# Layer 1's projections formed inside layer 0's finish, and the branch to the general path placed behind layer 1

## The chip, the cores and the metric

The kernel runs on one core of one Trainium2 chip. The metric is the device time of one execution in microseconds (us), and less is better. A core has a matrix engine (TensorE, "PE" in the profile, with "PEld" for its weight loads), VectorE (DVE), ScalarE (ACT), GpSimd (POOL) and a sequencer for transfers (SyncE, "SP"). Each engine works through its own queue in order, and the engines wait for each other by semaphores. Transfers (DMA) are issued from the queues of SP, ACT and POOL.

## The reference

There are N = 2708 nodes with D = 256 features and a weighted adjacency matrix `adj`. Two layers follow each other, and each is wrapped as `x = layernorm(x + layer(x))`.

Layer 0 walks two steps over the graph and attends two steps with nucleus sparsification:

```
R = (S + I) / rowsum
for n in 0, 1:
    A  = top-p attention of Xa          # softmax(q k^T), the fewest entries with 0.9 of the mass, renormalised
    Xf = R @ Xf
    Xa = A @ Xa
    Z  = Z + Xf @ U1[n].T + Xa @ U2[n].T
out = layernorm(X + Z) * g + b
```

Layer 1 is graph attention with H = 4 heads of 64 features each:

```
Wh  = x @ W                      # per head
s_i = Wh . a_src,  s_j = Wh . a_dst
e   = leaky_relu(s_i + s_j, 0.2),  only where adj != 0 or i == j
out = softmax_j(e) @ Wh
```

The kernel writes exp(leaky_relu(s_i + s_j)) as a product: exp(s_j) times the larger of exp(0.8 s_i) and exp(-0.8 s_j), leaving out a factor that the softmax cancels. So layer 1 needs, for each node j, the values `Wh` scaled by exp(s_j), the number exp(s_j) itself for the denominator, the number `tj` = exp(-0.8 s_j), and the source score s_i.

## The kernel before

The nodes are cut into NT = 22 tiles: 16 of 128 rows and 6 of 110 rows. The features of all nodes lie in `xe` in SBUF for the whole run. Everything is in 32-bit floats.

**Layer 0** is `fast_layer0`. It runs step 0 and then step 1 of attention, one row tile after the other, in the function `step`. For each row tile, `weigh` (line 132) goes over six groups of up to four tiles: it transposes a group of the attention row on TensorE into the PSUM buffer `tr` (pool `ps_tr`, two buffers), copies it on ScalarE to `eT`, and multiplies it with the values (line 157). After each group, `slot` lets other work in. It first advances the searches for coming rows (`going`), then the tails of earlier rows (`doing`), and then spends a number of matmuls on the walk `R @ Xf` (line 783). The order of the four compute engines inside this part is the order in which the Python code emits it (`tc.manual_schedule`). The order on SP, and the place of everything outside that region, are chosen by the framework's list scheduler, which goes by program order and by its own estimate of when things are ready.

A search for row tile t (`search`) computes the scores and their exponentials, finds a threshold with tallies on ScalarE (line 583) and small arithmetic on GpSimd, and on VectorE picks candidates (line 663), sorts them and cuts the row `e` (line 732).

The tail of a row tile in step 1 is `finish` (lines 848 to 883). It sums the terms on GpSimd, applies two layernorms (VectorE and GpSimd in turn), and writes the new features into `xe` (line 873). It is a generator; each `yield` gives the engines a slot.

After layer 0 a number `bad` tells whether the fast search was valid for every row. Line 1030 loads it into a register of each engine, and a branch (line 1031) enters `general_layer0` if it is positive. With these inputs the branch is not entered. A conditional block splits the program: nothing traced behind it can be scheduled ahead of it.

**Layer 1** begins with a loop of its own over the 22 tiles (lines 1053 to 1081). Per tile it makes two transposes of `xe` (line 1060), a copy on ScalarE (line 1064), two matmuls with `wx` (W and the two score vectors side by side, 264 columns, line 1067), two exponentials on ScalarE (lines 1072 and 1073), a copy and a product on VectorE (lines 1076 and 1077) and a copy on GpSimd that spreads exp(s_j) over 32 columns (`bj`, line 1081). `targets(g)` (lines 1089 to 1104) turns the source scores of a span of eight tiles into the rows `r`. `neighbours(g, j)` loads a block of `adjT`, and makes a mask of zeros and ones with ScalarE (Sign, line 1112), GpSimd (two products on the diagonal block, lines 1115 and 1116) and ScalarE again (Square, line 1117). The main loop runs over three spans and 22 tiles j: four VectorE instructions make `pt` (line 1164), and TensorE multiplies them with `v` (line 1172) and with `bj` (line 1179) into six PSUM banks. At the end of a span `settle` divides, adds `xe` and applies the last layernorm.

Pools of SBUF and PSUM are stacked. A pool of layer 1 lies on bytes of released pools of layer 0, and the framework lets all of its tiles wait for every user of the pools on whose bytes it lies. In layer 0 the pools stand in this order: `w0` (weights), `rowp` (small per-row buffers, among them `xT` and `cs`, two buffers each), `keep`, `sortp`, `heldp` (with `hh`, which `finish` uses), `finp`, `ep` and others. In layer 1 they are `keep1` (`v`, `bj`; it lies on `w0`, `rowp` and the start of `keep`), `pp`, `rp` (`r`; by its size it ends on `heldp`), `adjp1` (the blocks `bar`; on `heldp`, `finp` and `ep`) and `pj` (`pt`).

Of the kernel before, what the change touches and what calls it, by code (L numbers as in the profile page):

```python
# [45 lines left out]
def kernel(  # L46
# [36 lines left out]
    const = ctx.enter_context(tc.tile_pool(name="const", bufs=1))  # L83
# [24 lines left out]
    nc.vector.tensor_scalar(offdiag, ident, -1.0, 1.0, op0=ALU.mult, op1=ALU.add)  # L108
    minus_half = const.tile([P, 1], F32, name="minus_half")
    nc.gpsimd.memset(minus_half, -0.5)  # L110
    bad = const.tile([1, 1], I32, name="bad")

    def load_x():
# [4 lines left out]
    def layernorm(dst, src, m):  # L118

        st = small.tile([P, 6], F32, name="ln_st")  # L120
        nc.vector.bn_stats(st[:m], src)
        mv = small.tile([P, 2], F32, name="ln_mv")
        nc.vector.bn_aggr(mv[:m], st[:m])
        ve = small.tile([P, 1], F32, name="ln_ve")
        nc.gpsimd.tensor_scalar(ve[:m], mv[:m, 1:2], LN_EPS, None, op0=ALU.add)  # L125
        rs = small.tile([P, 1], F32, name="ln_rs")
        nc.gpsimd.tensor_tensor(rs[:m], ve[:m], minus_half[:m], op=ALU.pow)
        nc.vector.tensor_scalar(  # L128
            dst, src, mv[:m, 0:1], rs[:m], op0=ALU.subtract, op1=ALU.mult
        )  # L130

    def weigh(acc, e, m, value, pool, ps, copies, between=None):

# [31 lines left out]
    def general_layer0():  # L165
        with ExitStack() as l0:
# [232 lines left out]
            for s in range(STEPS):  # L399
                cur = xe if s == 0 else xa1  # L400
                ahead = scores(s, 0)
                for t in range(NT):
                    m = rows[t]
                    e, tau = ahead
                    if t + 1 < NT:
                        ahead = scores(s, t + 1)
                    if s == 0:
                        xf, xa = xf1[:, t, :], xa1[:, t, :]
                    else:
                        xf = rowp.tile([P, D], F32, name="xf2")  # L410
                        xa = rowp.tile([P, D], F32, name="xa2")
                    walk(s, t, xf[:m])
                    rden = top_p(t, e, tau)
                    attend(t, e, rden, cur, xa[:m])
                    if s == 0:
                        project(1, t, xa)
                    else:
                        finish(t, xf, xa)


    def fast_layer0():
# [426 lines left out]
        def finish(t, ac, ca, cb):  # L848

            m = rows[t]  # L850
            xt = xe[:m, t, 0:D]
            xw = rowp.tile([P, D], F32, name="xw")[:m]
            nc.scalar.activation(xw, ac[:m, :D], AF.Copy, scale=rinv[:m, t : t + 1])  # L853
            yield
            while t not in held:
                yield
            hh = heldp.tile([P, D], F32, name="hh", bufs=4)[:m]
            nc.gpsimd.tensor_add(ca[:m], ca[:m], cb[:m])
            nc.gpsimd.tensor_add(ca[:m], ca[:m], held.pop(t)[:m])
            nc.gpsimd.tensor_add(hh, ca[:m], xw)  # L860
            yield
            for last in range(2):
                st, mv = small.tile([P, 6], F32, name="ln_st")[:m], small.tile([P, 2], F32, name="ln_mv")[:m]
                nc.vector.bn_stats(st, hh)
                nc.vector.bn_aggr(mv, st)
                yield
                yield
                ve, rs = new("ln_ve", m), new("ln_rs", m)
                nc.gpsimd.tensor_scalar(ve, mv[:, 1:2], LN_EPS, None, op0=ALU.add)
                nc.gpsimd.tensor_tensor(rs, ve, minus_half[:m], op=ALU.pow)  # L870
                yield
                yield
                nc.vector.tensor_scalar(
                    xt if last else hh, hh, mv[:, 0:1], rs, op0=ALU.subtract, op1=ALU.mult
                )
                yield
                yield
                if not last:
                    nc.gpsimd.tensor_mul(hh, hh, g_sb[:m])
                    nc.gpsimd.tensor_add(hh, hh, b_sb[:m])  # L880
                    nc.gpsimd.tensor_add(hh, hh, xt)
                    yield
                    yield


        engines = {nc.tensor.engine, nc.scalar.engine, nc.vector.engine, nc.gpsimd.engine}
# [139 lines left out]
        )  # L1026
        l0.close()

    fast_layer0()
    flag = nc.values_load(bad[0:1, 0:1])  # L1030
    with tc.If(flag > 0):
        general_layer0()

    with ExitStack() as l1:  # L1040
        keep = l1.enter_context(tc.tile_pool(name="keep1", bufs=1))
        pp = l1.enter_context(tc.tile_pool(name="pp", bufs=2))
        GT = 8
# [1 line left out]
        GW = GT * rows[0]  # L1045


        v = keep.tile([P, NT, H, FO], F32, name="v")
        bj = keep.tile([P, NT, H, 32], F32, name="bj")
        tj = keep.tile([P, NT, H], F32, name="tj")  # L1050
        s_src = keep.tile([P, NT, H], F32, name="s_src")

        with ExitStack() as pre:
            ps_x = pre.enter_context(tc.tile_pool(name="ps_x", bufs=2, space=PSUM))
            ps_w = pre.enter_context(tc.tile_pool(name="ps_w", bufs=2, space=PSUM))
            for t in range(NT):
                m = rows[t]
                tp = ps_x.tile([P, DC, P], F32, name="tp")
                for c in range(DC):
                    nc.tensor.transpose(  # L1060
                        tp[:, c, :m], xe[:m, t, c * P : (c + 1) * P], ident[:m, :m]
                    )
                xT = pp.tile([P, DC, P], F32, name="xT")
                nc.scalar.copy(xT[:, :, :m], tp[:, :, :m])
                wp = ps_w.tile([P, D + 2 * H], F32, name="wp")
                for c in range(DC):
                    nc.tensor.matmul(
                        wp[:m], xT[:, c, :m], wx[:, c, :],
                        start=(c == 0), stop=(c == DC - 1),
                    )  # L1070
                b = small.tile([P, H], F32, name="b_j")
                nc.scalar.activation(b[:m], wp[:m, D : D + H], AF.Exp)
                nc.scalar.activation(
                    tj[:m, t, :], wp[:m, D : D + H], AF.Exp, scale=NEG_SLOPE - 1.0
                )
                nc.vector.tensor_copy(s_src[:m, t, :], wp[:m, D + H : D + 2 * H])
                nc.vector.tensor_tensor(
                    v[:m, t], wp[:m, 0:D].rearrange("p (h o) -> p h o", h=H),
                    b[:m].unsqueeze(2).to_broadcast([m, H, FO]), op=ALU.mult,
                )  # L1080
                nc.gpsimd.tensor_copy(bj[:m, t], b[:m].unsqueeze(2).to_broadcast([m, H, 32]))

        rp = l1.enter_context(tc.tile_pool(name="rp", bufs=2))
        adjp = l1.enter_context(tc.tile_pool(name="adjp1", bufs=4))
# [61 lines left out]
        for g, span in enumerate(spans):  # L1146
# [6 lines left out]
            for j in range(NT):  # L1153
                k = rows[j]
                if j == 2 and due:
                    settle(*due)
                if j == NT // 2 and g + 1 < len(spans):
                    r_next = targets(g + 1)
                mask = neighbours(g, j)
                at = dict(start=(j == 0), stop=(j == NT - 1), skip_group_check=True)  # L1160
                pts = []
                for h in range(H):
                    pt = pj.tile([P, GW], F32, name=f"pt{h}")
                    nc.vector.scalar_tensor_tensor(  # L1164
                        pt[:k, :gw], r[:k, h, :gw], tj[:k, j, h : h + 1], mask,
                        op0=ALU.max, op1=ALU.mult,
                    )
                    pts.append(pt)
                    if h % 2 == 1:
                        for c, (c0, w) in enumerate(cuts):  # L1170
                            for q in range(2):
                                nc.tensor.matmul(  # L1172
                                    acc[h // 2][c][q * FO : (q + 1) * FO, :w],
                                    v[:k, j, h - 1 + q, :],
                                    pts[h - 1 + q][:k, c0 : c0 + w], **at,
                                )
                for c, (c0, w) in enumerate(cuts):
                    for h in range(H):
                        nc.tensor.matmul(  # L1179
                            acc[2][c][h * 32 : (h + 1) * 32, :w],  # L1180
                            bj[:k, j, h, :], pts[h][:k, c0 : c0 + w], **at,
                        )
            r = r_next
            val = pp.tile([P, 2, GW], F32, name="val")
# [4 lines left out]
                nc.scalar.copy(den[:, c0 : c0 + w], acc[2][c][:, :w])  # L1189
            due = (g, val, den)  # L1190
        settle(*due)


# [43 lines left out]
```

## Time and profile before

Three runs gave 1730.11, 1731.68 and 1733.36 us. The profiled execution took 1728.95 us, and its span from first to last instruction is 1727.2 us.

| engine | busy us | share of the span |
|---|---|---|
| PE (matmuls) | 1622.7 | 94% |
| DVE | 1230.5 | 71% |
| ACT | 752.6 | 44% |
| POOL | 441.6 | 26% |

The shares are means over stages with different limits. The stages follow each other like this (times from the timeline):

| stage | from us | to us |
|---|---|---|
| layer 0, step 0 and the change to step 1 | 0 | 671 |
| layer 0, step 1, up to the last row's cut attention row | 671 | 1280 |
| layer 0, last row's attention and its finish | 1280 | 1306 |
| branch | 1306 | 1310 |
| layer 1, own loop over tiles | 1310 | 1347 |
| layer 1, main loop | 1347 | 1708 |
| layer 1, last settle and end | 1708 | 1727 |

A line of the timeline has: start in us, duration in us, engine, line of the code, operation, output<-inputs, shape, and how many instructions of that kind were merged into it; in square brackets, how long the engine had been idle and what ended that. A letter q behind an engine (DVEq, SPq) means its sequencer: waits, branches, DMA issues. A table of windows has, for each stretch: its length, the busy time of PE, PEld, DVE, ACT and POOL with the number of instructions, the granted TensorE clock, the DMA share and GB/s. A line of the waits has: who waited, for whom, the sum in us, how often, the longest.

### The profile page before, as it was taken

To read this page: it belongs to the slowest core of one execution; us is meant where nothing else is said; L and a number is where in the kernel's file an instruction comes from. 1 tells how busy PE (TensorE), PEld (TensorE's weight loads), DVE (VectorE), ACT (ScalarE), POOL (GpSimd) and SP (SyncE) were. 2 spreads that over 40 slices of the span, in tenths; PEclk is the share of its full clock that TensorE was granted. 3 is DMA by queue.
4 is the path that set the end of the run, shared out by engine and by line. 5 is a ranking of instruction groups with operands and counts; after the bars stand their busy time and mean duration, and the time that the engine had idled before them with its cause. 6 is when DMAs were issued, how large, how long until landed. Compare 5 with 4: busy or idle time off the path is not lost. (4 is left out here: it accounts for less than half of the span.)

```text
span 1727.2 us, 24421 instructions
## 1 busy us (share of the span) xinstructions
PE 1622.7 (94%) x8434; PEld 1075.6 (62%) x8434; DVE 1230.5 (71%) x3725; ACT 752.6 (44%) x1235; POOL 441.6 (26%) x915
## 2 busy tenths in 40 slices
PE   5799999999999998999999999999886999999896
PEld 4577777777777776777787877777675322222332
DVE  2654455554455009888989999999972888898796
ACT  1233333333332236666675666566514343333231
POOL 0011111111110124323343434343433200430303
PEclk9999999999999999999999999999998999999998
DMA  6111011111111142222232233232201232232231
GB/s 161 33 45 48 22 42 42 42 30 36 42 39 42 41 106 65 58 63 58 73 81 74 77 77 78 71 73 54 63 16 51 74 89 88 83 98 79 69 87 36
DMA packets 147812, 108.34 MB, mean 63 GB/s; under 512 B 39254, under 2 KB 138034, under 8 KB 147682
## 3 DMA queue, kind: packets, MB, share of 16 engines
q1 hardware_dynamic: 142018, 99.11, 21.6%
q0 software_dynamic: 2112, 5.55, 0.9%
q10 hardware_dynamic: 3552, 2.07, 0.5%
q8 instruction: 68, 1.11, 0.3%
q14 instruction: 62, 0.51, 0.1%
HBM read 98.38 MB, written 8.32 MB: 62 GB/s over the span
## 5 line engine op out<-in xcount | busy, mean ns | idle before, releaser
L1164 DVE SCALAR_TENSOR_TENSOR pt<-r,tj,bar 128x1024 f32<-128x1024 f32 (+3 forms) x264 | 295.9, 1181 | 29.2 <-issue 19.0
L583 ACT ACTIVATE junk<-e,minus,rth 128x2708 bf16<-128x2708 f32 (+1 forms) x88 | 232.8, 2645 | 39.8 <-POOL rth L615 36.6
L783 PE MATMUL walk<-xe,blk 128*128 128x257 f32 (+3 forms) x968 | 243.1, 385 | 0.0
L157 PE MATMUL att<-xe,eT 128*128 128x256 f32 (+3 forms) x968 | 233.4, 381 | 7.6 <-ACT eT L148 7.6
L157 PE MATMUL att<-ba,eT 128*128 128x256 f32 (+3 forms) x968 | 234.1, 383 | 5.0 <-ACT eT L148 5.0
L783 PE MATMUL walk<-yw,blk 128*128 128x256 f32 (+3 forms) x968 | 229.3, 383 | 4.0 <-ACT xw L853 4.0
L1172 PE MATMUL acc<-pt,v 128*64 128x512 f32 (+3 forms) x1056 | 228.3, 550 | 3.8 <-DVE pt L1164 3.8
L148 ACT COPY eT<-tr 128x512 f32<-128x512 f32 (+5 forms) x264 | 136.8, 536 | 212.3 <-PE tr L142 212.0
L783 PEld LDWEIGHTS walk<-xe,blk 128*128 128x128 f32 (+3 forms) x968 | 173.2, 187 | 64.8 <-issue 41.8
L783 PEld LDWEIGHTS walk<-yw,blk 128*128 128x128 f32 (+3 forms) x968 | 177.0, 186 | 51.6 <-issue 18.1
L663 DVE MAX8 cand<-e 128x8 f32<-128x170 f32 (+1 forms) x352 | 89.4, 322 | 146.3 <-ACT e L562 146.3
L157 PEld LDWEIGHTS att<-xe,eT 128*128 128x128 f32 (+3 forms) x968 | 170.9, 186 | 35.8 <-ACT eT L148 12.6
L157 PEld LDWEIGHTS att<-ba,eT 128*128 128x128 f32 (+3 forms) x968 | 171.9, 187 | 33.3 <-ACT eT L148 10.3
L562 ACT ACTIVATE e<-lg 128x1024 f32<-128x1024 f32 (+1 forms) x132 | 121.0, 921 | 132.7 <-PE lg L558 127.8
L1172 PEld LDWEIGHTS acc<-pt,v 128*64 128x64 f32 (+1 forms) x1056 | 72.4, 136 | 152.7 <-issue 110.8
L142 PE MATMUL tr<-ident,e 128*128 128x128 f32 (+3 forms) x968 | 138.7, 269 | 15.0 <-DVE e L732 13.7
L142 PEld LDWEIGHTS tr<-ident,e 128*128 128x128 f32 (+3 forms) x968 | 115.3, 139 | 42.3 <-issue 16.3
L1112 ACT ACTIVATE bar<-bar 128x1024 f32<-128x1024 f32 (+3 forms) x66 | 63.0, 955 | 152.6 <-DMA bar<-in_adjT_dram 138.5
L1179 PE MATMUL acc<-pt,bj 128*32 128x512 f32 (+3 forms) x1056 | 125.6, 549 | 0.0
L796 DVE TENSOR_TENSOR xf<-walk,xe 128x257 f32<-128x257 f32 (+1 forms) x22 | 9.4, 426 | 157.0 <-PE walk L783 156.9
L663 DVE MAX8 cand<-scr 128x8 f32<-128x97 f32 (+1 forms) x616 | 101.7, 243 | 0.0
L681 DVE MAX8 top<-work 128x8 f32<-128x128 f32 (+3 forms) x242 | 82.3, 340 | 8.3
(194 smaller groups left out, 1980.8 us busy)
## 6 DMA issues: line engine op xcount, KB each, us to landing
blk<-in_adjT_dram SPq DMA_DIRECT2D x32, 704.0 KB
bar<-in_adjT_dram SPq DMA_DIRECT2D x32, 512.0 KB
blk<-in_adjT_dram SPq DMA_DIRECT2D x32, 330.0 KB
blk<-in_adjT_dram SPq DMA_DIRECT2D x32, 320.0 KB
blk<-in_adjT_dram SPq DMA_DIRECT2D x12, 605.0 KB
bar<-in_adjT_dram SPq DMA_DIRECT2D x12, 440.0 KB
bar<-in_adjT_dram SPq DMA_DIRECT2D x16, 330.0 KB
c<-cs POOLq DMA_DIRECT2D x32, 128.0 KB, 2.9
```

The lines of the kernel that those rows point to most:

```text
L142: nc.tensor.transpose(tr[: rows[t], q, :m], e[:m, off[t] : off[t + 1]], ident[:m, :m])
L148: copy(eT[:k, : len(grp), :m], tr[:k, : len(grp), :m])
L157: nc.tensor.matmul(acc, eT[: rows[t], q, :m], value(t), start=(t == 0), stop=(t == NT - 1),)
L562: nc.scalar.activation(halves[:m, :, c0 : c0 + w], lg[:m, :, :w], AF.Exp, accum_out=zp[:m, n : n + 1],)
L583: nc.scalar.activation(junk[:m], e[:m], func, scale=rth, bias=minus1[:m], accum_out=acc)
L663: nc.vector.max(cand[:, n, :], src[:m, n * size : min(N, (n + 1) * size)])
L681: nc.vector.max(top[:, k : k + 8], work if k else flat)
L783: nc.tensor.matmul(ac[:m, :w], blk[: rows[j], j - j0, :m], cur[: rows[j], j, 0:w], start=(j == 0), stop=(j == NT - 1),)
L1112: nc.scalar.activation(bar, bar, AF.Sign)
L1164: nc.vector.scalar_tensor_tensor(pt[:k, :gw], r[:k, h, :gw], tj[:k, j, h : h + 1], mask, op0=ALU.max, op1=ALU.mult,)
L1172: nc.tensor.matmul(acc[h // 2][c][q * FO : (q + 1) * FO, :w], v[:k, j, h - 1 + q, :], pts[h - 1 + q][:k, c0 : c0 + w], **at,)
L1179: nc.tensor.matmul(acc[2][c][h * 32 : (h + 1) * 32, :w], bj[:k, j, h, :], pts[h][:k, c0 : c0 + w], **at,)
```

## The change

A new generator `sources(t, pool, ps)` makes, for one tile, what layer 1's own loop made: transposes, `xT`, two matmuls with `wx`, two exponentials (now into `sb` and `tj`, which with `s_src` moved into the `const` pool), the copy of the source scores, and the values. The copy moves from VectorE to ScalarE. The product with exp(s_j) moves from one VectorE instruction of 256 columns to four ScalarE instructions of 64 columns with a per-row scale. The values go to a DRAM tile `vd[t]` by a transfer on SP. It uses the `tr` buffers of `ps_tr` and the buffers `xT` and `cs` of `rowp`.

`finish` ends with `yield from sources(t, rowp, ps_tr)`, so it runs inside the hand-ordered region. The general path calls it for all tiles at its end.

Layer 1 becomes a function. In place of its loop it loads the values of each tile from DRAM by a transfer on ACT's queue, and GpSimd spreads `sb` into `bj`. It is called right behind `fast_layer0`; the branch follows, and its arm holds the general layer 0 and a second copy of layer 1.

```diff
+    sb, tj, s_src = (const.tile([P, NT, H], F32, name=k) for k in ("sb", "tj", "s_src"))
+    kept = ctx.enter_context(tc.tile_pool(name="kept", bufs=1, space=bass.MemoryType.DRAM))
+    vd = [kept.tile([P, D], F32, name=f"v_{t}") for t in range(NT)]
...
+    def sources(t, pool, ps):
+        m = rows[t]
+        tp = ps.tile([P, 4, P], F32, name="tr")
+        for c in range(DC):
+            nc.tensor.transpose(tp[:, c, :m], xe[:m, t, c * P : (c + 1) * P], ident[:m, :m])
+        xT = pool.tile([P, DC, P], F32, name="xT")
+        nc.scalar.copy(xT[:, :, :m], tp[:, 0:DC, :m])
+        yield
+        wp = ps.tile([P, 4, P], F32, name="tr").rearrange("p a b -> p (a b)")
+        for c in range(DC):
+            nc.tensor.matmul(
+                wp[:m, : D + 2 * H], xT[:, c, :m], wx[:, c, :],
+                start=(c == 0), stop=(c == DC - 1),
+            )
+        nc.scalar.activation(sb[:m, t, :], wp[:m, D : D + H], AF.Exp)
+        nc.scalar.activation(tj[:m, t, :], wp[:m, D : D + H], AF.Exp, scale=NEG_SLOPE - 1.0)
+        nc.scalar.copy(s_src[:m, t, :], wp[:m, D + H : D + 2 * H])
+        vt = pool.tile([P, D], F32, name="cs")
+        for h in range(H):
+            cols = slice(h * FO, (h + 1) * FO)
+            nc.scalar.activation(
+                vt[:m, cols], wp[:m, cols], AF.Copy, scale=sb[:m, t, h : h + 1]
+            )
+        nc.sync.dma_start(vd[t][:m], vt[:m])
...
+            yield from sources(t, rowp, ps_tr)      # at the end of finish
...
-    fast_layer0()
-    flag = nc.values_load(bad[0:1, 0:1])
-    with tc.If(flag > 0):
-        general_layer0()
-    with ExitStack() as l1:
+    def layer1():
+        l1 = ExitStack()
...
-        v = keep.tile([P, NT, H, FO], F32, name="v")
-        bj = keep.tile([P, NT, H, 32], F32, name="bj")
...
-            for t in range(NT):
...
-                nc.vector.tensor_copy(s_src[:m, t, :], wp[:m, D + H : D + 2 * H])
-                nc.vector.tensor_tensor(
-                    v[:m, t], wp[:m, 0:D].rearrange("p (h o) -> p h o", h=H),
-                    b[:m].unsqueeze(2).to_broadcast([m, H, FO]), op=ALU.mult,
-                )
-                nc.gpsimd.tensor_copy(bj[:m, t], b[:m].unsqueeze(2).to_broadcast([m, H, 32]))
+        v = [keep.tile([P, H, FO], F32, name=f"v{t}") for t in range(NT)]
+        bj = [keep.tile([P, H, 32], F32, name=f"bj{t}") for t in range(NT)]
+        for t in range(NT):
+            m = rows[t]
+            nc.scalar.dma_start(v[t][:m].rearrange("p h o -> p (h o)"), vd[t][:m])
+            nc.gpsimd.tensor_copy(
+                bj[t][:m], sb[:m, t, :].unsqueeze(2).to_broadcast([m, H, 32])
+            )
...
+    fast_layer0()
+    layer1()
+    flag = nc.values_load(bad[0:1, 0:1])
+    with tc.If(flag > 0):
+        general_layer0()
+        layer1()
```

More of the change, by code (lines that the diff above doesn't have):

```diff
@@ L418, in general_layer0 @@
                         finish(t, xf, xa)
+            for t in range(NT):
+                for _ in sources(t, rowp, ps_tr):
+                    pass
     def fast_layer0():
@@ L1045 @@
         GW = GT * rows[0]
-        v = keep.tile([P, NT, H, FO], F32, name="v")
-        bj = keep.tile([P, NT, H, 32], F32, name="bj")
[L1050 to L1055, printed above, removed]
-            for t in range(NT):
[L1057 to L1061, printed above, removed]
-                    )
[L1063 to L1075, printed above, removed]
-                nc.vector.tensor_copy(s_src[:m, t, :], wp[:m, D + H : D + 2 * H])
-                nc.vector.tensor_tensor(
-                    v[:m, t], wp[:m, 0:D].rearrange("p (h o) -> p h o", h=H),
-                    b[:m].unsqueeze(2).to_broadcast([m, H, FO]), op=ALU.mult,
-                )
-                nc.gpsimd.tensor_copy(bj[:m, t], b[:m].unsqueeze(2).to_broadcast([m, H, 32]))
+        v = [keep.tile([P, H, FO], F32, name=f"v{t}") for t in range(NT)]
+        bj = [keep.tile([P, H, 32], F32, name=f"bj{t}") for t in range(NT)]
+        for t in range(NT):
+            m = rows[t]
[3 more added lines that the diff above has]
+            )
         rp = l1.enter_context(tc.tile_pool(name="rp", bufs=2))
@@ L1173 @@
                                     acc[h // 2][c][q * FO : (q + 1) * FO, :w],
-                                    v[:k, j, h - 1 + q, :],
+                                    v[j][:k, h - 1 + q, :],
                                     pts[h - 1 + q][:k, c0 : c0 + w], **at,
@@ L1180 @@
                             acc[2][c][h * 32 : (h + 1) * 32, :w],
-                            bj[:k, j, h, :], pts[h][:k, c0 : c0 + w], **at,
+                            bj[j][:k, h, :], pts[h][:k, c0 : c0 + w], **at,
                         )
@@ L1191 @@
         settle(*due)
+        l1.close()
+    fast_layer0()
[4 more added lines that the diff above has]
+        layer1()
 _ARGS = [
```

## The prediction, made before the changed kernel was run

> **What bounds the kernel now.** I read first the table of windows, because the change touches three stages with different limits: layer 0's step 1 while rows are being finished, the hand-over from layer 0 to layer 1, and the end.
>
> ```profile
> 877.00:1277.40 400.40, 384.53 (x1884) 300.61 (x1882) 379.87 (x1415) 238.04 (x314) 164.87 (x383) 1.00 0.27 68
> 1277.40:1296.40 19.00, 15.44 (x76) 12.16 (x76) 8.52 (x20) 3.82 (x8) 7.42 (x8) 0.91 0.00 0
> 1296.40:1309.60 13.20, 0.00 (x0) 0.00 (x0) 3.46 (x9) 0.00 (x0) 7.94 (x14) 0.56 0.02 6
> 1309.60:1347.00 37.40, 35.24 (x178) 27.38 (x179) 12.63 (x46) 24.68 (x85) 9.67 (x30) 0.93 0.17 57
> 1347.00:1707.00 360.00, 353.95 (x2191) 110.46 (x2194) 316.08 (x348) 127.05 (x146) 70.05 (x84) 1.00 0.28 82
> ```
>
> From 877 to 1277 PE is busy 384.5 of 400.4 us and DVE 379.9: two full engines, and PE has only 15.9 us to spare. This is where `finish` runs: its last instruction (L873, output `xe`) occurs 22 times, from 883.5 to 1305.9. From 1296.4 to 1309.6 PE does nothing. From 1309.6 to 1347.0 it does layer 1's own loop and the first `targets`. The main loop behind is PE's (354 of 360).
>
> Next, who makes PE wait in step 1 (window 670 to 1296 of the waits):
>
> ```profile
> PE tr L142 <- DVE e L732: 13.7, 10, 4.6
> PE att L157 <- ACT eT L148: 5.0, 21, 0.2
> PE walk L783 <- ACT xw L853: 4.0, 3, 1.7
> ```
>
> Of the 13.7 us for the cut row `e`, 2.16 fall on row 0, 4.59 on the last row and 6.95 on eight rows between. Last, the hand-over in the timeline, and the issues of transfers and the branch:
>
> ```profile
> 1305.90 0.42 DVE L873 TENSOR_SCALAR xe<-hh,ln_mv,ln_rs 110x256 f32<-110x256 f32 x1 [1.00 <-POOL ln_rs L870]
> 1309.70 1.09 PE L1060 MATMUL tp<-ident,xe 128*128 128x128 f32 x4 [13.71 <-DVEq L1031]
> 1310.96 3.86 PE L1067 MATMUL wp<-wx,xT 128*128 128x264 f32 x8 [0.17 <-ACT xT L1064]
> ...
> 1315.74 2.05 PE L1067 MATMUL wp<-wx,xT 128*128 128x264 f32 x8
> 1317.62 0.60 PE L1060 MATMUL tp<-ident,xe 128*128 128x128 f32 x4
> 1318.06 0.49 PE L1097 MATMUL aux<-ident,s_src 128*128 128x128 f32 x3
> ...
> 1345.31 14.44 DVE L1164 SCALAR_TENSOR_TENSOR pt<-r,tj,bar 128x1024 f32<-128x1024 f32 x12
> ...
> 1347.02 2.75 PE L1172 MATMUL acc<-pt,v 128*64 128x512 f32 x8
> ...
> L1031 DVEq COMPARE_BRANCH  x1: 76/76/76, 1306.5 to 1306.5; - x1
> L1031 DVEq EVENT_SEMAPHORE  x1: 21/21/21, 1309.4 to 1309.4; - x1
> ...
> L1111 SPq DMA_DIRECT2D bar<-in_adjT_dram x66: 291/328/695, 1309.6 to 1690.2; - x66
> ```
>
> The reader is to see a serial piece: the last row's attention ends at 1295.9 (ACT's `xa`, L921), its layernorms at 1306.3, DVE leaves the branch at 1309.4, and the main loop's first matmul starts at 1347.0. That is 51.1 us from `xa` to `acc`.
>
> **What the Trainium skill says.** "Runtime: NRT & Kernel Launch", Instruction fetch mechanics: a taken branch to a target outside the fetched pages stalls for the fetch. The trace agrees: DVE's branch takes 0.08 us, and its next instruction comes 2.9 us later. "DMA: Bandwidth & Descriptors", Anatomy of one DMA, gives each transfer a fixed cost of about 2 us, mostly the receipt of the write. Its figure is for GpSimd's path; the trace's `c<-cs`, 128 KB on POOL's queue, lands in 2.0 to 4.0 us, median 2.3. "TensorE: Matmul & The Clock Gate", What's actually happening, says the array idles to half clock. The trace agrees: eight records of L1067 span 3.65 us right behind the gap (next group at 1314.61), 1.88 later. "ScalarE: Activation LUTs", What ACT_TABLE_LOAD costs, prices the new form below.
>
> **The change part by part.**
>
> Added to PE, per tile: four records of L1067 are 1.88/2 = 0.94 us (1315.74 to 1317.62 is two tiles); two transposes are 0.44/2 = 0.22. So 1.16 us. Finishes of rows 0 to 18 end before 1277: 19 × 1.16 = **22.0 us** in the stage where PE has 15.9 to spare. Which part of that can be filled? The waits for `e` (6.95), since a later PE meets a row that is ready; DVE gets no new work in the stage. Waits for `eT` right behind them stay. 22.0 − 6.95 = +15.1. In the last row come rows 19 and 20, 2.3 us, against a wait of 4.59 for `e` that should go too: −2.3.
>
> Added to ACT, per tile: `xT` of 128x256, 0.37 us by the same copy at L544; two exponentials and a copy of 4 columns, 0.17 each in the trace and about 0.1 apart; four copies of 64 columns with a scale per row, which no row shows. The skill's ScalarE page gives 186 ns plus 0.83 ns a column, 93 more for an operand per row, and 93 of overlap: an estimate of 0.24 us each. Below by the trace: 0.17 (four columns); above: 0.46 (256 columns with a scale). I take 0.24. Sum 0.37 + 0.3 + 0.96 = 1.6 us, 31 us in 19 rows, on an engine busy 238 of 400. Queued behind them on ACT are the next `eT` copy, a tally (2.65 us) and `xw`. The `eT` copy has a whole group of PE's work (about 4 us) before it is needed, but `xw` gates PE: the walk has one PSUM buffer. Three such waits cost 4.0 now. I add 2 (bounds 0 and 21, see rival B). `tr` has two buffers and `wp` holds one for some 2 us; the next transposes use the other. No cost.
>
> Sum up to the last `xa`: 15.1 − 2.3 + 2 = **+15 us**.
>
> SP gets 22 issues of `vd` at 0.33 us, in line with the `blk` loads. Their three buffers are fetched half a walk ahead, several us, which hides it. GpSimd and DVE get nothing there.
>
> Removed at the hand-over: the branch ahead of layer 1 (3.3 us from 1306.3) and its loop. What remains behind the last `xa`: `finish` of row 21, 10.4 us as before (1295.9 to 1306.3), then three chains.
> (a) `sources(21)`: transposes 0.25, `xT` 0.37, matmuls 0.94 to 1.9 (cold clock), seven ACT instructions 1.3, hand-offs about 0.5, so 4; `vd` written at +0.3 issue +2.3 = about 7. `v` lies on `rowp`, whose users include this tile's `cs` with its transfer, so all loads of `v` wait for it: v[0] is there at 7 + 0.33 + 2.3 = 9.6.
> (b) `r` and the first `bar` lie partly on `heldp`, whose last user is L864 of row 21, so they too start at 1306.3. ACT then owes eight exponentials of L1101 at 0.60 = 4.8, the 1.7 of sources(21), and Sign and Square of the first mask, 2.1: 8.6 serial.
> (c) ACT also issues the 22 loads of `v` at about 0.33 (SP's median; ACT's single issue of 256 KB took 0.35) = 7.3 us, during which masks stand still, and GpSimd makes 22 copies `bj` at 0.29 = 6.4.
> If the first mask comes ahead of the loads, DVE starts at about 9 and PE 1.7 later (1345.31 to 1347.02), but mask 1 comes at about 18 where DVE wants it at 14. If behind, DVE starts at 16 and PE at 17.6. So the loop starts between 10 and 20 us behind `xe`, and I take 15. `targets`' transposes lie beside this.
> 10.4 + 15 = 25.4 in place of 51.1: **−25.7 us**.
>
> Added at the end: register load, branch and fetch behind the last layernorm. From DVE's last instruction (1723.1) to the span's end are 4.1 us, in which the last output lands; SP's own stall of about 3 us lies beside that landing in part. Bounds 0 and 5; I take **+2**.
>
> Main loop: the same instructions, 0.
>
> Sum: 15 − 25.7 + 2 = −8.7 on the span of 1727.2, so 1718.5 there. The runs shown stand at 1731.68 (median); I carry the difference over: **1723.0 us**.
>
> **The rivals.**
> A, more is hidden: step 1 pays only 9 (PE's idle 15.9 nearly all filled), the first two masks come ahead of the loads of `v` and the loop starts at 10, the end costs 1. 9 − 30.7 + 1 = −20.7: 1711. For it: DVE has 95%, so its rows set part of the pace. Against: 5.0 us of the idle are `eT` hand-offs.
> B, slower: the new ACT work lands ahead of `xw`. PE then waits for the walk's only PSUM buffer, 1.6 us a time as at the longest of now, in 16 of 19 walks instead of 3: 13 × 1.6 = 20.8, of which my sum holds 2. −8.7 + 18.8 = +10.1: 1742. It turns the sign from about seven further waits on ((8.7 + 2)/1.6). For it: L853 waits behind tallies already. Against: ACT is 60% busy, and the sources come late in `finish`, in a slot of their own.
> C, given back at the start: the 22 issues and 22 `bj` copies all precede the masks' work, and 2.8 MB of `v` share the DMA engines with the blocks. The loop starts at 23 instead of 15. −0.7: 1731. In this form the change doesn't do what it says, since the loop's time returns as a wait.
>
> **How the numbers follow.** The forecast has 0.50 (own range 1716 to 1730), A 0.17, B 0.18, C 0.15. A measurement of this kernel tells about 0.2% (3.5 us) from no change. Faster by more: 0.45 of the forecast's and A's 0.17, 0.62. Within: 0.05 and 0.12 of C, 0.17. Slower: B's 0.18 and 0.03 of C, 0.21. The range goes from 1709 to 1738: it leaves out a third of A, 0.05, and most of B, 0.13, and little else.
>
> **What would show it.** Step right if: from 877 on the rows' period grows by about 1.2 us (17.1 us over 14 rows) and PE's waits for `e` L732 shrink below 3 us in sum; `xw` waits stay under 8 us; from the last `xa` to the first `acc` are 20 to 30 us, with ACT holding 22 issues near its start; DVE's last instruction is followed by 5 to 7 us. Wrong if the last `xa` comes more than 25 us later (B), or the first masks wait behind the loads beyond 20 us from `xe` (C), or the scheduler puts the loads of `v` or `r` otherwise than by these pools.

## The result and the profile after

Beside the kernel before on the same chip, the changed kernel took 1722.34 us (median of four runs, 1721.0 to 1723.0) against 1731.23 (1730.11 to 1733.36). The ratio is 0.9946, with a 95% interval of 0.9929 to 0.9963. The span of the profiled execution is 1720.4 us, 6.8 less than the 1727.2 of before. The medians differ by 8.9, because the profiled execution of before was 2.3 us faster than the median there.

Three moments cut both executions at the same places: ACT's last `xa` (the end of layer 0's attention), the first matmul into `acc` (the start of layer 1's main loop), and DVE's last instruction. Starts are meant; the last 0.41 us instruction is left out of "end".

| | last xa | xa to first acc | acc to DVE's last | from there to the end | span |
|---|---|---|---|---|---|
| before | 1295.9 | 51.1 | 375.7 | 4.1 | 1727.2 |
| after | 1304.4 | 31.8 | 377.2 | 6.6 | 1720.4 |
| difference | +8.5 | -19.3 | +1.5 | +2.5 | -6.8 |

The table of windows of the changed kernel, for the same step 1 stretch as before, the hand-over and the main loop:

```profile
877.00:1277.40 400.40, 395.30 (x1961) 312.92 (x1960) 373.96 (x1389) 260.42 (x449) 171.40 (x380) 1.00 0.28 74
1318.00:1336.20 18.20, 6.08 (x34) 4.67 (x32) 1.37 (x2) 7.55 (x17) 6.37 (x25) 0.69 0.79 251
1336.20:1696.00 359.80, 353.75 (x2185) 111.59 (x2187) 316.90 (x347) 132.53 (x152) 73.63 (x90) 0.99 0.28 82
```

In step 1 PE is busy 395.3 of 400.4 us instead of 384.5: its idle time went from 15.9 us to 5.1, so two thirds of it were filled. In the second line PE is busy for a third of 18 us. PE's waits in step 1 show what was filled:

```profile
PE att L187 <- ACT eT L178: 5.0, 21, 0.3
PE tr L172 <- DVE e L765: 4.9, 2, 2.7
PE walk L816 <- ACT xw L886: 1.7, 3, 0.8
```

The wait for the cut row `e` fell from 13.7 us to 4.9, the wait for `xw` from 4.0 to 1.7, and the hand-offs of `eT` stayed at 5.0. The timeline of the hand-over:

```profile
1304.37 0.47 ACT L955 ACTIVATE xa<-att,rden 110x256 f32<-110x256 f32 x1 [1.42 <-PE att L187]
...
1314.38 0.42 DVE L906 TENSOR_SCALAR xe<-hh,ln_mv,ln_rs 110x256 f32<-110x256 f32 x1 [1.00 <-POOL ln_rs L903]
...
1321.19 1.07 ACT L1105 ACTIVATE r<-aux 128x512 f32<-128x512 f32 x2
1321.90 10.82 ACTq L1082 DMA_DIRECT2D v<-v  x22
1332.77 1.09 ACT L1105 ACTIVATE r<-aux 128x512 f32<-128x512 f32 x2 [10.50 <-DMA v<-v]
1333.73 1.06 ACT L1121 ACTIVATE bar<-bar 128x1024 f32<-128x1024 f32 x1
1334.83 27.82 DVE L1168 SCALAR_TENSOR_TENSOR pt<-r,tj,bar 128x1024 f32<-128x1024 f32 x21 [20.03 <-DMA v<-v]
1336.17 6.21 PE L1176 MATMUL acc<-pt,v 128*64 128x512 f32 x16 [0.78 <-DVE pt L1168]
```

ACT issues the 22 loads of `v` from 1321.9 to 1332.7. The last two of the eight exponentials of `r` and the Square that finishes the first mask stand behind them in ACT's queue, and DVE's first `pt` needs both. The profile names the landing of `v` as what ended DVE's wait, but `pt` reads `r`, `tj` and `bar` only; the Square ends at 1334.79, 0.04 us ahead of `pt`. Last, the end of the run, where the branch now is:

```profile
1713.38 0.41 DVE L132 TENSOR_SCALAR o<-res,ln_mv,ln_rs 110x256 f32<-110x256 f32 x1 [1.34 <-DMA out_dram<-o]
...
L1201 DVEq COMPARE_BRANCH  x1: 76/76/76, 1714.0 to 1714.0; - x1
L1201 DVEq EVENT_SEMAPHORE  x1: 21/21/21, 1717.2 to 1717.2; - x1
...
L1200 SPq TENSOR_LOAD <-bad x1: 672/672/672, 1714.2 to 1714.2; - x1
```

DVE branches at 1714.0 and goes on at 1717.2, as it did at 1306.5 and 1309.4 before. The stall was not removed, it was moved to where 4.1 us of landing output cover part of it.

### The profile page after: what moved, and what is told of

Its sections match the earlier page's. It is cut to its first block, busy times and chain, and to the rows that moved or that the text cites. A ratio compares the mean times of both kernels' runs of the same rounds, so it can differ in the third digit from the quotient of the medians.

```text
span 1720.4 us, 24503 instructions
## 1 busy us (share of the span) xinstructions
PE 1624.2 (94%) x8434; PEld 1080.7 (63%) x8434; DVE 1221.5 (71%) x3681; ACT 771.1 (45%) x1345; POOL 450.9 (26%) x915
## 4 chain that ended last, share of the span: by engine, by line
PE 70%; DVE 15%; ACT 6%; POOL 4%; DMA 2%; issue 2%; ACTq 0%; SPq 0%; POOLq 0%; DVEq 0%
PE att L187 20%; PE walk L816 16%; PE acc L1176 11%; PE acc L1183 6%; PE lg L591 4%; PE tr L172 3%; ACT e L595 3%; PE tr L559 2%; DVE cand L696 2%; PE tr L872 2%; PE tr L852 2%; DVE scr L762 2%; DVE e L765 1%; DVE scr L681 1%; DVE work L716 1%
## 5 line engine op out<-in xcount | busy, mean ns | idle before, releaser
L616 ACT ACTIVATE junk<-e,minus,rth 128x2708 bf16<-128x2708 f32 (+1 forms) x88 | 232.8, 2646 | 33.5 <-POOL rth L648 32.7
```

Of the source, the lines that this page charges most:

```text
L616: nc.scalar.activation(junk[:m], e[:m], func, scale=rth, bias=minus1[:m], accum_out=acc)
```

## Experiments

All ratios are to the kernel before on the same chip, with 95% intervals. One caution for spans of single executions: the first `xa` of step 1, at which no edit has acted yet, lies between 701.0 and 705.0 us in the executions shown here, so spans carry some 2 us of drift to either side. Where an edit acts late, the distance from the last `xa` is the sharper reading.

| run | last xa | xa to acc | acc to DVE's last | span | median | ratio |
|---|---|---|---|---|---|---|
| branch behind, own loop kept | 1295.8 | 41.1 | 372.4 | 1716.6 | 1718.44 | 0.9943 [0.9925, 0.9961] |
| sources in finish, branch between | 1304.1 | 43.2 | 376.8 | 1728.8 | 1730.07 | 1.0001 [0.9992, 1.0010] |
| changed kernel without the branch | 1304.4 | 32.7 | 377.6 | 1719.1 | 1719.06 | 0.9936 [0.9919, 0.9953] |
| keep1 behind pp | 1304.7 | 35.9 | 377.8 | 1725.8 | 1725.54 | 0.9976 [0.9967, 0.9985] |
| v loaded by SP | 1302.8 | 23.7 | 377.0 | 1710.7 | 1713.17 | 0.9906 [0.9889, 0.9922] |
| v by SP, when due | 1302.5 | 23.8 | 378.0 | 1711.3 | 1713.42 | 0.9908 [0.9892, 0.9925] |
| the same, keep1 behind pp | 1301.5 | 25.0 | 377.7 | 1711.8 | 1715.65 | 0.9923 [0.9906, 0.9939] |
| sources' TensorE work twice | 1318.2 | 21.7 | 386.0 | 1733.3 | 1735.73 | 1.0035 [1.0020, 1.0049] |
| sources' ScalarE work twice | 1306.8 | 23.4 | 385.8 | 1723.2 | 1720.82 | 0.9951 [0.9934, 0.9967] |
| v when due, r early | 1303.3 | 18.9 | 379.7 | 1709.2 | 1710.84 | 0.9891 [0.9874, 0.9907] |
| the same, bj made in finish | 1299.8 | 21.3 | 375.9 | 1704.2 | 1706.79 | 0.9874 [0.9857, 0.9890] |

In the two runs with doubled work ACT's order came out otherwise: the first mask stands ahead of the loads of `v`, so the main loop starts sooner and then waits. There the sum of both columns compares (407.7 and 409.2, against 409.0 of the changed kernel).

### The two halves of the change, each alone

Own loop of layer 1 kept as before, only the branch behind it (edit against the kernel before):

```diff
     fast_layer0()
-    flag = nc.values_load(bad[0:1, 0:1])
-    with tc.If(flag > 0):
-        general_layer0()
-    ...            # layer 1 with its own loop over tiles
+    layer1()       # the same layer 1 with its own loop over tiles
+    flag = nc.values_load(bad[0:1, 0:1])
+    with tc.If(flag > 0):
+        general_layer0()
+        layer1()
```

> Layer 1 keeps its own loop over the tiles, and only the branch moves behind it. My theory: step 1 is untouched, so the last xa stays at 1295.9 us. Without the branch between, the loop over tiles 0 to 20 can fill PE's 13 us gap behind it, so from xa to the first acc are about 38 us in place of 51.1, and the end grows by 2.5: span about 1717, 10 below the kernel before. That would mean that the branch's place brings as much as the whole change. Rival: the gain of the whole change comes from the moved projections; then the loop starts no earlier, because its buffers wait for layer 0's pools, and the span is 1724 to 1730.

Sources in `finish`, values by DRAM, but the branch between the layers (edit against the changed kernel, as in all further runs):

```diff
     fast_layer0()
-    layer1()
     flag = nc.values_load(bad[0:1, 0:1])
     with tc.If(flag > 0):
         general_layer0()
-        layer1()
+    layer1()
```

> The projections are moved into finish as in the changed kernel, and the branch stands between the layers as before. My theory: last xa at about 1304.4 as in the changed kernel; the branch opens at about 1323 behind sources(21); then 22 issues of v on ScalarE (about 10.8 us), exponentials and masks: first acc at about 1342, end 2.5 shorter than in the changed kernel: span about 1724. Rival (the branch's place is worth nothing beside the moved projections): span 1718 to 1721.

The branch alone has a ratio of 0.9943, which can't be told from the 0.9946 of the whole change; its span is even 3.8 us shorter (1.2 of it drift). The sources alone bring nothing: 1.0001. So the place of the branch carries the whole of the measured gain, and moving the projections, with the loads of `v` on ACT's queue, costs about what it saves. That was in no rival of the prediction. For the branch alone, the timeline says where it comes from:

```profile
1295.84 0.47 ACT L921 ACTIVATE xa<-att,rden 110x256 f32<-110x256 f32 x1 [2.20 <-PE att L157]
1296.21 0.64 ACT L1054 COPY xT<-tp 128x256 f32<-128x256 f32 x2
1296.68 2.02 PE L1057 MATMUL wp<-wx,xT 128*128 128x264 f32 x8 [0.75 <-ACT xT L1054]
```

Layer 1's own loop now begins under the last row's layernorms, 0.4 us behind `xa`, because nothing splits the program there. The first `acc` comes 41.1 us behind `xa`, where about 38 were expected. The span of 1717 is met because the main loop is also 3.3 us shorter, which was not expected. Of these, 1.9 lie in its first tile: it takes 5.4 us (1336.91 to 1342.35) instead of 7.4 (1347.02 to 1354.39), and DVE had made its `pt` ahead, from 1328.2 on. The rest stays open. For the sources alone, the timeline says why no gain is left:

```profile
1321.51 1.97 PE L1101 MATMUL aux<-ident,s_src 128*128 128x128 f32 x8 [3.59 <-ACTq L1200]
1321.86 5.32 SPq L1115 DMA_DIRECT2D bar<-in_adjT_dram  x4
1321.90 5.17 POOL L1083 COPY bj<-sb 128x128 f32<-128x128 f32 x22 [7.80 <-SPq L1200]
1324.08 13.93 ACTq L1082 DMA_DIRECT2D v<-v  x22
1338.06 1.08 ACT L1105 ACTIVATE r<-aux 128x512 f32<-128x512 f32 x2 [18.96 <-DMA v<-v]
```

Behind the branch all 22 loads of `v` come ahead of all exponentials of `r`. The first `acc` is at 1347.3, as before (1347.0). From PE's first instruction behind the branch to `acc` are 25.8 us (1321.5 to 1347.3) where layer 1's own loop took 37.3 (1309.7 to 1347.0), so 11.5 are saved. But the last `xa` comes 8.2 later, and from `xa` to that first instruction are 17.4 us instead of 13.8, since the last tiles' sources now stand behind `xe`. The account is even. Both expectations for this run missed.

### The end without the branch

```diff
     fast_layer0()
     layer1()
-    flag = nc.values_load(bad[0:1, 0:1])
-    with tc.If(flag > 0):
-        general_layer0()
-        layer1()
```

This leaves out the general path for rows on which the fast search isn't valid.

> The changed kernel without the branch and its arm: the general path, which these inputs do not enter, is left out. My theory: only the end changes; from DVE's last instruction to the span's end are 4.1 us as before in place of 6.6: span 2.5 below the changed kernel's 1720.4, about 1718. Rival: the branch's wait lies beside the landing of the output: less than 1 us.

From DVE's last instruction to the end are 4.0 us instead of 6.6, so the branch at the end costs 2.6. The span fell by only 1.3, as the loop started 0.9 us later and took 0.4 more, for a reason that stays open.

### What delays the main loop: buffers, or ACT's queue

First the pools alone: `pp` is opened ahead of `keep1`, so `v` and `bj` no longer lie on `rowp`.

```diff
-        keep = l1.enter_context(tc.tile_pool(name="keep1", bufs=1))
         pp = l1.enter_context(tc.tile_pool(name="pp", bufs=2))
+        keep = l1.enter_context(tc.tile_pool(name="keep1", bufs=1))
```

> The changed kernel with the two pools pp and keep1 opened in the other order, so that v and bj lie on bytes of keep alone, whose last user is the last row's attention, and not on rowp, which sources(21) uses. My theory (the loads of v wait for rowp's last user and then hold up ScalarE for 10.8 us): the loads are issued from about 1305 on, beside row 21's finish, except for v of tile 21; first acc at about 1326 in place of 1336.2: span about 1710 to 1712. Rival (the loop's start is set by r and the first mask, which wait for heldp's last user anyway): less than 3 us of gain, span above 1717.

The theory missed clearly, since this run is slower than the changed kernel (0.9976); the rival's numbers are met, though it did not foresee a loss. The loads do start early, at 1304.9, but only eight of 22 can be issued before 1319, because ACT works in order and stands waiting for row 20's `xT` in between. The other 14 come from 1319.5 to 1331.1, and now all eight exponentials of `r` are behind them:

```profile
1315.69 0.34 ACT L143 COPY xT<-tr 128x220 f32<-128x220 f32 x1 [7.94 <-PE tr L141]
...
1322.91 8.18 ACTq L1082 DMA_DIRECT2D v<-v  x10
1331.13 1.09 ACT L1105 ACTIVATE r<-aux 128x512 f32<-128x512 f32 x2 [7.97 <-DMA v<-v]
```

GpSimd's copies `bj` moved forward as well, in between row 21's own operations, and the last `xe` comes 13.6 us behind `xa` instead of 10.0. So the next run takes the issues away from ACT and leaves all else. It was made after the run with `v` loaded when due, which stands below it, in order to part that run's two edits:

```diff
-            nc.scalar.dma_start(v[t][:m].rearrange("p h o -> p (h o)"), vd[t][:m])
+            nc.sync.dma_start(v[t][:m].rearrange("p h o -> p (h o)"), vd[t][:m])
```

> The changed kernel with one edit: the 22 loads of v are issued by SyncE instead of ScalarE, at the same place; the copies bj stay. Theory (ScalarE's 10.8 us of issues in front of the last exponentials of r and the first mask are the whole of what the run with v loaded when due gained): the first acc comes 23 to 25 us after the last xa instead of 31.8, span 1711 to 1714, equal to that run within 2 us. Rival (that run gained by the later place of loads and copies): xa to acc stays above 28 us, span 1717 or more.

One word in the code takes 8.1 us off the way from `xa` to `acc` (31.8 to 23.7), and the ratio goes to 0.9906. The last `xa` is 1.6 us earlier besides, with the first at the same place, and why is open. From the timeline of this run:

```profile
1319.68 10.27 SPq L1082 DMA_DIRECT2D v<-v  x22
...
1321.65 1.06 ACT L1105 ACTIVATE r<-aux 128x512 f32<-128x512 f32 x2
...
1322.82 27.84 DVE L1168 SCALAR_TENSOR_TENSOR pt<-r,tj,bar 128x1024 f32<-128x1024 f32 x19 [9.59 <-DMA bar<-in_adjT_dram]
1326.54 1.05 PE L1183 MATMUL acc<-pt,bj 128*32 128x512 f32 x2 [3.12 <-DMA v<-v]
```

The issues take as long on SP (10.27 us), but nobody waits behind them, and ACT finishes `r` in their time. Loading `v` and copying `bj` at the steps that need them adds nothing to this:

```diff
+        def fetch(t):        # v[t] by nc.sync, bj[t] by GpSimd
...
                 mask = neighbours(g, j)
+                if g == 0:
+                    for t in range(j + 3 if j else 0, min(j + 4, NT)):
+                        fetch(t)
```

> The changed kernel, but the loads of v are issued by SyncE instead of ScalarE, and each load and its copy bj comes at its own step of the first span's loop, three steps ahead of its use (the first four behind mask 0). Theory (22 issues on ScalarE, 10.8 us, ahead of the last exponentials of r and the first mask set the loop's start): the first acc comes at about 1325 to 1328 instead of 1336.2 and the span is 1709 to 1713. Rival (the start is set by the release of row 21's buffers, the landing of v and the exponentials of r): the first acc comes no earlier than 1332 and the span is 1716 or more.

It meets the theory's numbers (1326.3, 1711.3), but equals the run with SP alone, so they came from the queue alone. The list scheduler moves the copies forward anyhow, as soon as their buffers are free:

```profile
1320.33 7.21 POOL L1084 COPY bj<-sb 128x128 f32<-128x128 f32 x22
```

With the pools in the other order too:

> As the run with v loaded when due, and the two pools opened in the other order, so that v and bj no longer lie on buffers that row 21 uses to its end. Theory (with the issues off ScalarE and the copies bj at their steps, the early place of v is at last worth something): the first loads land before row 21 is done, the first acc at 1323 to 1326, the span 1707 to 1711, 0 to 3 us below the run without it. Rival (it moves other tiles onto those buffers, as before when it cost 5.4 us): not below that run.

The rival was right: nothing is gained (25.0 against 23.8). The copies `bj` come between row 21's layernorms again, and a VectorE instruction that takes 0.41 us in the changed kernel takes 1.38 beside them:

```profile
1307.86 1.61 POOL L1084 COPY bj<-sb 128x128 f32<-128x128 f32 x6
1307.94 1.38 DVE L906 TENSOR_SCALAR hh<-hh,ln_mv,ln_rs 110x256 f32<-110x256 f32 x1 [0.31 <-POOL ln_rs L903]
```

The Trainium skill, "SBUF — State Buffer", SBUF: two separate sides, says that GpSimd and some VectorE instructions share a pair of ports as an exclusive lock, so that one of them stands still. These two lines agree: the six copies and the 1.38 us start and end together within 0.2 us. That the lock is the cause is argued from this, and no run took it apart.

### The price of the moved projection in step 1

All of TensorE's part of `sources` issued twice into the same PSUM tile:

```diff
-        for c in range(DC):
-            nc.tensor.transpose(tp[:, c, :m], ...)
+        for _ in range(2):
+            for c in range(DC):
+                nc.tensor.transpose(tp[:, c, :m], ...)
...
+        for c in range(DC):
+            nc.tensor.matmul(wp[:m, : D + 2 * H], ...)     # the two matmuls once more
```

> The changed kernel, but every tile's two transposes and two matmuls of the moved projection are issued twice over into the same PSUM tile; ScalarE's work and all transfers stay as they are. Theory (TensorE's idle time between 877 and 1277 us paid for most of the first copy; 15.9 us shrank to 5.1): a second copy of 1.16 us a tile finds nothing left to fill, so 21 tiles cost 20 to 24 us on the last xa (1304.4 becomes about 1326), plus 1 to 2 us for tile 21 behind it: span about 1743. Rival (the stage's pace is set by VectorE's rows and by hand-offs, TensorE's work lies beside them): the second copy costs no more than the first, 8 to 9 us, span 1728 to 1731.

And ScalarE's part (copy of `xT`, two exponentials, copy of `s_src`, four scaled copies) twice:

> The changed kernel, but ScalarE's part of the moved projection (copy of xT, two exponentials, copy of s_src, four scaled copies) is issued twice over, some 1.7 us a tile; TensorE's work and the transfers stay. Theory (ScalarE, 260 of 400 us busy, has the slot free): the last xa moves by less than 4 us, and the hand-over takes about 2 us more for tile 21: span 1721 to 1726. Rival (ScalarE's queue delays xw and eT, for which TensorE waits): the last xa moves by 10 us or more, span 1732 or more, with waits of TensorE for xw and eT grown by as much.

TensorE's second copy moved the last `xa` by 13.9 us, between the two numbers. The rows' own times decide. These are the 14 rows of step 1 from row 6's `xa` to row 20's, in the kernel before, with one copy and with two; the projections of 18 tiles lie in them:

```profile
879.56:1274.26 394.70, 380.28 (x1865) 297.57 (x1866) 374.34 (x1394) 236.75 (x311) 163.42 (x381) 1.00 0.27 68
879.90:1283.20 403.30, 398.20 (x1973) 315.32 (x1974) 376.89 (x1404) 260.75 (x456) 172.60 (x381) 1.00 0.27 73
878.45:1300.54 422.09, 417.81 (x2081) 332.62 (x2082) 382.03 (x1406) 261.75 (x456) 178.96 (x381) 1.00 0.26 70
```

The first copy adds 17.9 us of PE's busy time (1.00 a tile) and the rows take 8.6 longer, since PE's idle time falls from 14.4 us to 5.1. The second adds 19.6 and the rows take 18.8 longer, as only 0.8 us of idle time goes. The last row gives 3.5 us back (17.7 against 21.2 us) and 1.5 are drift. Of the 3.5, 2.7 are in the wait for `e`:

```profile
PE tr L178 <- DVE e L771: 2.2, 1, 2.2
```

That is 2.2 us where one copy leaves 4.9. The theory holds for the rows, and missed the sum because of the last one, and because 19 tiles' work, not 21's, lies ahead of the last `xa`. ScalarE's second copy moved the last `xa` by 2.4 us, of which 1.3 are drift, and the ratio by less than its interval. So the price in step 1 is TensorE's, and ScalarE's work there is hidden.

### A version ahead of both

The pool `pp` moves behind the pools of `r` and the masks, so that these lie on layer 0's `qT`, `yw` and `ba`, which are free earlier:

```diff
         keep = l1.enter_context(tc.tile_pool(name="keep1", bufs=1))
-        pp = l1.enter_context(tc.tile_pool(name="pp", bufs=2))
...
         rp = l1.enter_context(tc.tile_pool(name="rp", bufs=2))
         adjp = l1.enter_context(tc.tile_pool(name="adjp1", bufs=4))
+        pp = l1.enter_context(tc.tile_pool(name="pp", bufs=2))
```

> As the run with v loaded when due, and the pool pp (needed only when a span of targets is done) is opened behind the pools of r and of the masks, so that r and the masks of the first span lie on layer 0's qT, yw and ba instead of on sortp and heldp. Theory (what holds r and the first mask until row 21's second layernorm is the buffers they lie on; their data, rows 0 to 7 and adjT, are there long before): the exponentials of r start right behind the last xa, the first acc comes 14 to 18 us after xa (23.8 without), as soon as VectorE has left row 21, and the span is 1701 to 1706. Rival (PSUM banks of row 21's own projection, or v and bj on row 21's buffers, hold the loop as long): xa to acc stays above 21 us, span 1708 or more.

The loop starts 18.9 us behind `xa`, sooner by 4.8, and so neither in the theory's range (14 to 18) nor in the rival's (above 21). But the loop itself is 1.7 longer, and the span lands in the rival's range. The third mask is late:

```profile
1331.26 1.46 POOL L1083 COPY bj<-sb 128x128 f32<-128x128 f32 x6
1331.34 1.06 ACT L1122 ACTIVATE bar<-bar 128x1024 f32<-128x1024 f32 x1 [7.92 <-POOL bar L1121]
1332.43 7.94 DVE L1172 SCALAR_TENSOR_TENSOR pt<-r,tj,bar 128x1024 f32<-128x1024 f32 x6 [1.69 <-ACT bar L1122]
```

ACT waits 7.9 us for GpSimd, whose copies `bj` stand between the masks' operations. So `bj` is made in each row's `finish` and travels with `v`:

```diff
+        wide = pool.tile([P, H, 32], F32, name="wide", bufs=1)
+        nc.gpsimd.tensor_copy(wide[:m], sb[:m, t, :].unsqueeze(2).to_broadcast([m, H, 32]))
-        nc.sync.dma_start(vd[t][:m], vt[:m])
+        nc.sync.dma_start(vd[t][:m, :D], vt[:m])
+        nc.sync.dma_start(vd[t][:m, D:], wide[:m].rearrange("p h o -> p (h o)"))
...
+            nc.sync.dma_start(vb[t][:m], vd[t][:m])
```

> As the run with r early, and bj is formed by GpSimd inside each row's finish and kept behind v in the same DRAM tile, so that layer 1 loads both with one transfer and makes no copies at its start. Theory (in the run with r early the loop started 4.8 us sooner after xa, but kept only about 2 us of it, because GpSimd's copies bj came between the first masks' own two operations): the second and third mask come without a wait, the gain of the start is kept, span 1704 to 1707. Rival (ScalarE's own order in the hand-over, exponentials of r between the first masks, is what spends it, and v and bj still wait for row 21's buffers): span 1708 to 1712, and a longer last xa if GpSimd's copies disturb the rows.

1706.79 us, a ratio of 0.9874. Its interval and that of the run before overlap, as do those of that run and of the two with `v` on SP, so what follows on these last two steps rests on single traces. The waits of that kind are gone (the mask in question now waits 1.42 us), and the loop is 3.8 us shorter. But the theory has only part of the credit. From `xa` to DVE's last instruction it is 1.4 us better than the run before, as PE now waits for `v` at the start, and 3.5 us are in the last `xa`: 0.6 of drift and 2.9 in step 1, which nothing in the theory explains and no run took apart.

```profile
1321.12 5.15 PE L1179 MATMUL acc<-pt,v 128*64 128x512 f32 x16 [3.55 <-DMA v<-v]
```

## Why the prediction was right, and where it was not

The time, 1723.0 forecast and 1722.34 measured, is right, and so are the steps' signs. That it is so close is luck: two of the terms in its sum were mis-sized by 6.5 us each, in opposite directions, and on the spans -8.7 were forecast and -6.8 came.

**Up to the last xa, +15.** It was +8.5, of which 0.4 are drift. For the rows, 22.0 of TensorE work less 6.95, and 2 for new waits for `xw`, make 17.1; the 14 rows took 8.6 more. The work was taken too large: 19 tiles at 1.16 us, where the trace has 18 at 1.00, 17.9 in all. And what could be filled was taken too small: the waits for `e` went whole, as foreseen (7.0 us in these rows; of the 4.9 left, 2.2 are row 0's and 2.7 the last row's), but those for `xw` fell by 2.3 (4.0 to 1.7) where 2 were added. 17.9 - 7.0 - 2.3 is 8.6. Rival A's 9 for step 1 comes near, but by filling 13 of 22.0. The last row gave back 0.5 us and not 2.3: its wait for `e` shrank from 4.6 and did not go, and of projections only row 18's lies there. Row 18's finish ends at 1281.0 already in the trace of before, not ahead of 1277, and the matmuls of rows 19 and 20 start at 1305.1 and 1312.5, behind the last `xa`. ScalarE's estimate, 0.24 us for each scaled copy, holds: the trace has four in 0.93. Rival B, that this work would hold up `xw`, falls: PE waits 1.7 us for `xw`, and 2.2 with that work done twice. One reading, on which no term hung, was of half the data: 2.3 us for the landing of `c<-cs` is the median of one of its two lines, and over both it is 2.9.

**From xa to acc, -25.7.** It was -19.3. Of this way, the 10.4 us to the last `xe` came out as foreseen. From there the prediction chose 15 us between 10 and 20; the trace has 21.4 from the end of `xe`. The timeline of the hand-over puts it in one place, ACT's stretch of issues. The 22 issues were priced at 0.33 us each, from loads of `bar`, and took 10.82/22 = 0.49. And the order was taken for open, where the scheduler put them ahead of the Square that finishes the first mask. For that order the prediction had 17.6 us; with 10.8 for the issues in place of 7.3 it would have had 21.1. This is in the main rival C's mechanism, at nearly its size (23), and the prediction's own sign of being wrong, 20 us from `xe`, was reached: the first `pt` starts 20.0 us behind the end of `xe`. Moving the same issues to SP gave 8.1 us back, so the cause is shown, not argued, and leaves 13.3 us from `xe`, inside the 10 to 20.

**The end, +2.** It was +2.5, and the run without the branch confirms it (2.6). **The main loop, 0.** It was +1.5. Its first 16 `acc` matmuls with `v` take 6.21 us and the next 16 take 3.65:

```profile
1334.00:1340.00 6.00, 5.22 (x15) 2.67 (x15) 5.17 (x4) 3.74 (x4) 4.03 (x4) 0.50 0.13 44
1340.00:1344.20 4.20, 4.20 (x28) 1.26 (x24) 4.20 (x4) 2.97 (x4) 2.01 (x3) 1.00 0.40 125
1344.16 3.65 PE L1176 MATMUL acc<-pt,v 128*64 128x512 f32 x16
```

The clock granted behind the mostly idle stretch was 0.50, and 1.00 from 1340 on, which agrees with the Trainium skill, "TensorE: Matmul & The Clock Gate", What's actually happening: an idle array runs slower. But DVE's first `pt` come one by one there too, and no run parts the two. The first tile takes 8.0 us up to the next tile's matmuls, 0.6 more than before (7.4); the other 0.9 us of the loop stay open.

**What the prediction did not see** is how the gain divides. It booked the hand-over as one step and credited the removed loop with most of it. The halves show otherwise: the branch's place alone is worth 10.6 us of span, because layer 1's loop then starts beside the last row's finish. With the sources moved as well, 8.5 us are paid in step 1 to remove a loop that had already found cover in part. The change was 3.8 us worse in span than its better half, which the measured ratios can't tell from equal. The moved sources pay once ACT doesn't issue the loads of `v`: with SP the ratio is 0.9906, against 0.9943 of the branch alone, and the intervals don't overlap. The sources with SP's loads and the branch between the layers were not run.

## What to carry to other kernels

A conditional between two stages cost more here than its stall, because nothing behind it could be placed ahead of it; move it away first, alone, and measure, before moving work across it. Count each DMA issue as time of the engine whose queue it is on, and keep long rows of them off an engine that others are waiting for: here one word, SyncE's queue for ScalarE's, took off another 0.4%, where the whole change had brought 0.5%. Work put into a stage that looked full cost half while idle time was left (8.6 of 17.9 us), and nearly its whole price after that (18.8 of 19.6), so ask of the stage's waits how much they can still take.

## What was not expected of the hardware

Transfers of 110 and 128 KB from DRAM to SBUF, 22 behind each other, held the queue of the issuing engine for 0.44 us each in the median on ACT (0.29 to 0.62) and 0.43 on SP, a third more than the 0.33 of the loads of `bar` on SP, of up to 512 KB, in the kernel before. Why is open. The register load in front of the branch at the end took 0.47 to 0.67 us by engine, and the branch stalled DVE for 2.9 us between the layers and 3.2 at the end.
